# The third delta projection of a scan job, moved behind the group sum on TensorE

## The chip, the cores and the metric

One core of a Trainium2 chip runs the whole network in one launch. The metric is the device time of that launch in microseconds. Three runs of the kernel before took 19326.3, 19345.53 and 19361.93 us; their median, 19345.53 us, is the time before.

## The reference, cut to what matters

The network has four layers. Three kinds of selective scan (Mamba) fill nearly all of its time: layer 0 (causal Mambas over whole images), layers 1 and 2 (scans of an image in four directions) and layer 3 (Mambas along rows and columns). Each of them computes, for every channel d and each of N = 16 states n, a recurrence along the tokens:

```
xdbl  = xc @ xpW.T                      # rank (6 or 12) delta rows, 16 B rows, 16 C rows
delta = softplus(dt @ dtW.T + dtB)      # the delta projection and its softplus
def step(h, t):
    d_t, u_t, b_t, c_t = t
    h = exp(d_t[..., None] * A) * h + (d_t * u_t)[..., None] * b_t[:, None, :]
    return h, sum(h * c_t[:, None, :], axis=-1)      # the sum over states
```

Batch 4, 48 x 48 tokens, 192 model channels, 384 channels inside a Mamba; all arithmetic is fp32. Around the scans stand input projections, short convolutions, gates, output projections, norms, a small convolution block between layers 0 and 1 and an MLP at the end.

## The kernel before, in words

**Jobs and groups.** A scan is cut into jobs of CH = 384 tokens and 384 channels (a direction of layers 1 and 2 has 192 channels; its job puts 2 x 8 of the 16 states on the two halves of the 128 partitions, `parts` = 2). A job has three channel blocks i = 0, 1, 2 and works on NG = 4 states at a time; the unit of work is a group (job, i, g). In layers 0 and 3 a job has 3 x 4 = 12 groups (`MambaJob`), in layers 1 and 2 it has 3 x 2 = 6 (`DirJob`). `run_jobs` (line 775) is called three times: for 96 jobs of layer 0, 192 jobs of layers 1 and 2 (the *scan layers* below), and 96 jobs of layer 3. Each call has 1152 groups.

**What a group costs.** Five steps, one or two on each engine:
- `decay` (393): four exps on ScalarE, a = exp(delta A). For the first block it first starts the loads of the B and C rows (`fetch`). There are three decay buffers, so the decays of group t+3 wait until the scan of group t has read its own.
- `scan` (431) on VectorE: a product b = du x B (the row `inputs<-du,bcb`) and the scan proper (`h<-a,inputs`). `gather` (108) puts all of their waits in front of the product: for the decays, for the C/B rows, for the copy of `du` when g = 0 (`pools.entered`), and for the readers of the h buffer that is to be overwritten (`pools.readers`, `pools.weighed`). There are `hbufs` h buffers: 3 in layer 0, 4 elsewhere.
- `weigh` (457) on GpSimd: h times C, in place.
- `reduce` (472) on TensorE: four matmuls with an identity (or, for `parts` = 2, with a 128 x 64 matrix that adds the halves) sum h over states into the PSUM tile y. With g = 0 the skip terms go first (`skip`).
- `enter` (426) on ScalarE: the copy of du = delta x for the next block into PSUM, once per block. It is passed to `decay` as `between` and comes before the fourth exp.

**The loop.** In `run_jobs`, iteration t of the main loop (805 to 847) issues the scan of group t, the decays of t+2 (`ahead`), the copy of a finished y on ScalarE (`take`), the weighing of t, then one slot of the *stream*, the side work (norms of the finished images, `Side`), the gate and du products on GpSimd, and last the sum over states of group t-1 (`behind`):

```
        stream.run(at if at < per - 1 else per)
        ...
        if 0 <= t - behind < len(groups):
            job, i, g = groups[t - behind]
            job.reduce(i, g)
```

`at` is the position of group t in its job, from 0 to `per` - 1 (11 or 5). TensorE, GpSimd, ScalarE and VectorE run their instructions in the order of this code (`InOrder`, `in_order`); only the DMA issues of SyncE are placed by the scheduler.

**The stream.** While job n is scanned, `Stream` (710) works off the *units* of job n+1: input projection, convolution, B/C projection (`bc`), three delta projections, gates, and the output projection of job n-1. A unit is a matmul part (`pe`) and a ScalarE part (`act`), each with the slot at which it may be issued. `Stream.run(slot)` issues units in list order, at most two matmul parts ahead of their ScalarE parts, since the units share two PSUM tiles `ps`: the third delta matmul takes the tile that the first delta's softplus has read.

**The deltas.** `projections` (344) makes the units concerned. `delta(i)` (358) is one matmul of 12 or 6 rows (`ps<-bcd,dtT`) and one softplus (`delta<-ps,vec`). All three have the same slot: position 7 in layer 0 and in the first of each pair of jobs of layer 3, position 5 in the second of a pair (the twin), position 2 in the scan layers. Softplus and exp lie in different activation tables, so that a table load stands before the first softplus and another after the last.

Of the kernel before, what the change touches and what calls it, by code (L numbers as in the profile page):

```python
# [308 lines left out]
class ScanJob:  # L309
# [34 lines left out]
    def projections(self, xs, *slots):  # L344

        k, nc, w, pools = self.k, self.k.nc, self.w, self.pools
        nr = 2 * N + w.rank
        W = pools.W

        def bc(px):  # L350
            self.bcd = k.tile(pools.two, [nr, W], "bcd", 1)
            if self.entry is not None:
                k.g.memset(self.bcd[:, self.entry : self.entry + 1], 0.0)
            k.copy(self.bcd[:, self.tokens], px)
            self.bc = k.dram([2 * N, W], "bc")
            nc.sync.dma_start(self.bc, self.bcd[: 2 * N, :])

        def delta(i):
            def act(pd):
                if i == 0:  # L360
                    self.delta = k.tile(pools.two, [128, 3, CH], "delta")
                k.act(self.delta[:, i, :], pd, AF.Softplus, bias=w.dtb[:, i, :])

            return self.unit(
                slots[1],
                128,
                lambda ps: (ps, [(w.dtT[2 * N : nr, i, :], self.bcd[2 * N : nr, self.tokens])]),
                act,
            )

        first = self.unit(
            slots[0],
            nr,
            lambda ps: (ps, [(w.xpT[:, i, :], xs()[: pools.wide, i, :]) for i in range(3)]),
            bc,
        )
        return first, [delta(i) for i in range(3)]

    def fetch(self, g):

# [394 lines left out]
def run_jobs(jobs, side=None):  # L775

    ahead, behind, taken, gated, driven = 2, 1, 2, 3, 3  # L780
    last_group = jobs[0].pools.groups - 1
    groups = [(job, i, g) for job in jobs for i in range(3) for g in range(last_group + 1)]
    per = len(groups) // len(jobs)

    def at_group(t, g):

        if 0 <= t < len(groups) and groups[t][2] == g:
            return groups[t][:2]

    def offer(job):  # L790
        if side is not None and job.steps is not None:
            side.waiting += job.steps()

    jobs[0].load()
    stream = Stream(jobs[0].units(None))
    for t in range(per):
        stream.run(t)
    for t in range(driven):
        if first := at_group(t, 0):
            first[0].drive(first[1])  # L800
    jobs[0].enter(0)
    for job, i, g in groups[:ahead]:
        job.decay(i, g)
    stream = Stream([])
    for t in range(len(groups) + gated):
        n, at = divmod(t, per)
        if at == 0:
            last = jobs[n - 1] if n else None
            if n + 1 < len(jobs):
                jobs[n + 1].load()  # L810
                stream = Stream(jobs[n + 1].units(last))
        if at == per - ahead:
            stream.run(at - 1)
        if at == taken + 3 and n + 1 == len(jobs) and n:
            Stream(jobs[n - 1].outputs(*[(0, 0)] * 3)).run(per)
        if t < len(groups):
            job, i, g = groups[t]
            job.scan(i, g)
        coming = at_group(t + 1, 0)
        if t + ahead < len(groups):  # L820
            job, i, g = groups[t + ahead]
            job.decay(i, g, (lambda: coming[0].enter(coming[1])) if coming else None)
        if done := at_group(t - taken, last_group):
            done[0].take(done[1])
        if t < len(groups):
            if t + 1 < len(groups):
                job, i, g = groups[t + 1]
                job.carry(i, g)
            job, i, g = groups[t]
            job.weigh(i, g)  # L830
        stream.run(at if at < per - 1 else per)
        if t < len(groups):
            for slot, extra in jobs[n].extras:
                if slot == at:
                    extra()
        if side is not None and t < len(groups):
            if n and at == jobs[n - 1].offered:
                offer(jobs[n - 1])
            side.slot(at)
            side.end()  # L840
        if done := at_group(t - gated, last_group):
            done[0].gate(done[1])
        if begun := at_group(t + driven, 0):
            begun[0].drive(begun[1])
        if 0 <= t - behind < len(groups):
            job, i, g = groups[t - behind]
            job.reduce(i, g)
    Stream(jobs[-1].outputs(*[(0, 0)] * 3)).run(per)
    offer(jobs[-1])

# [118 lines left out]
def layer0(k, pairs, wh, norm, outs):  # L969
# [3 lines left out]
    with ExitStack() as ctx:  # L973
# [60 lines left out]
        for i in range(2):  # L1034
            jobs[n + i * NCH - NCH + 1].extras = ws[1][i].extras()
        run_jobs(jobs, side)


# [329 lines left out]
def scan_layers(k, pool, layers, ends, ahead):  # L1368
# [4 lines left out]
    with ExitStack() as ctx:  # L1373
# [9 lines left out]
        for n, (weights, src) in enumerate(layers):  # L1383
            ws, diag = weights.ws, weights.diag
            steps = ends[n](normed, pool)
            for b in range(B):
# [21 lines left out]
                late = scan(2, 0)  # L1408
        passes.append(late)
        run_jobs([job for p in passes for job in p], side)  # L1410
        scans.close()
        normed.alone = True
# [162 lines left out]
def row_mambas(k, weights, sets):  # L1575

    with ExitStack() as ctx:
        pools = ScanPools(k, ctx, 1, True)  # L1580
        jobs = []
        for (there, back), (srcs, outs, prior) in zip(weights.pairs, sets):
            if jobs:

                jobs[-2].extras = [(1, there.enter)]
            for b in range(B):
                for c in range(NCH):
                    of = None, srcs[b], outs[b]
                    last = prior[b] if prior is not None else None
                    first = MambaJob(k, pools, there, c * CH, False, *of)  # L1590
                    jobs += [
                        first,
                        MambaJob(k, pools, back, c * CH, True, *of, twin=first, prior=last),
                    ]
        run_jobs(jobs)
# [277 lines left out]
```

## Time and profile before

| of the profiled execution | |
|---|---|
| span | 19325.4 us (the three timed runs: 19326.3 to 19361.93) |
| busy: TensorE, VectorE, ScalarE, GpSimd | 17368.5, 18080.4, 12819.5, 14759.7 us |
| product `inputs<-du,bcb` on VectorE | 3456 times, 1769 ns |
| scan `h<-a,inputs` on VectorE | 3456 times, 3359 ns |
| weighing `h<-h,bcb` on GpSimd | 3456 times, 3447 ns |
| exps `a<-delta,A` on ScalarE | 13824 times, 602 ns |
| softplus `delta<-ps,vec` on ScalarE | 1152 times, 579 ns |
| delta matmuls `ps<-bcd,dtT` on TensorE | 2304 records (two for each fp32 matmul), 550 ns |

By name: PE is TensorE (PEld its weight loads), DVE VectorE, ACT ScalarE, POOL GpSimd, SPq the queue of SyncE. Most rows of the profile have line L56 or L93, those of two helpers, so groups are told apart by their tiles, written out<-in. A fp32 matmul leaves two records in the trace: the sum over states of one group is eight records. Time in brackets in a timeline is the idle time of the engine before the row, with what ended it as the profile infers it; of several waits it names the one that came last by its own account.

Layer 0 lies at about 40 to 6160 us of the span, the convolution block at 6160 to 6630, the scan layers at 6630 to 12710, layer 3 at 12870 to 18870, and the MLP follows up to 19325.

### The profile page before, as it was taken

The numbers are of one execution on the slowest core, as the hardware profiler recorded it, in microseconds if no ns is written. First come the engines' busy times: TensorE is split into PE (matmuls) and PEld (weight loads), VectorE is DVE, ScalarE is ACT, GpSimd is POOL, SyncE is SP. The second block draws the span as 40 slices with busy tenths as digits, with TensorE's granted clock in tenths as the row PEclk, the third lists the DMA queues.
The fourth block names the chain that finished last, engine by engine and source line by source line (L and its number), as shares of the span: only waits on it lengthen the run. The fifth ranks groups of instructions, "written<-read, shape, count | busy, mean of one in ns | idle before, by whom it ended". The sixth has DMA issues, their size and how long they took to land.

```text
span 19325.4 us, 162699 instructions
## 1 busy us (share of the span) xinstructions
PE 17368.5 (90%) x48240; PEld 8258.1 (43%) x48240; DVE 18080.4 (94%) x7297; ACT 12819.5 (66%) x22582; POOL 14759.7 (76%) x10860
## 2 busy tenths in 40 slices
PE   8999999999998888888888888889999999999999
PEld 4544545444444323333333333334444444444444
DVE  9999999999998699999999999969999999999993
ACT  6767777666665466676666777766666666666663
POOL 7888888878886288888888888857777777777770
PEclk9999999999999989999999999989999999999999
DMA  3333333323332366666666666633222332333231
GB/s 116 117 118 111 120 117 120 119 102 119 108 113 89 99 139 142 152 147 150 153 146 147 140 150 148 142 109 110 107 106 104 107 112 105 109 110 112 103 108 47
DMA packets 500500, 2306.55 MB, mean 119 GB/s; under 512 B 76664, under 2 KB 334304, under 8 KB 347168
## 3 DMA queue, kind: packets, MB, share of 16 engines
q1 hardware_dynamic: 499616, 2296.14, 41.9%
q8 instruction: 387, 6.34, 0.1%
q14 instruction: 497, 4.07, 0.1%
HBM read 2103.60 MB, written 192.32 MB: 119 GB/s over the span
## 4 chain that ended last, share of the span: by engine, by line
DVE 41%; POOL 32%; PE 13%; issue 9%; ACT 3%; DMA 2%; SPq 0%; POOLq 0%; DVEq 0%; ACTq 0%
DVE h L56 27%; POOL h L56 25%; DVE inputs L56 14%; PE y L56 6%; PE ps L56 4%; POOL dus L56 2%; PE vps L128 2%; POOL state L56 1%; ACT a L93 1%; DMA bcb<-bc 1%; POOL yt L56 1%; POOL bcb L56 1%; PE mop L128 1%; PE mps L128 1%; POOL nx L56 1%
## 5 line engine op out<-in xcount | busy, mean ns | idle before, releaser
L56 POOL TENSOR_TENSOR h<-h,bcb 128x1536 f32<-128x1536 f32 x3456 | 11912.3, 3447 | 1595.4 <-DVE h L56 1136.8
L56 DVE TENSOR_TENSOR_SCAN h<-a,inputs 128x1540 f32<-128x1540 f32 (+1 forms) x3456 | 11607.0, 3359 | 145.2 <-DVE inputs L56 1.4
L93 ACT ACTIVATE a<-delta,A 128x384 f32<-128x384 f32 (+1 forms) x13824 | 7417.2, 602 | 2662.1 <-DVE h L56 2642.6
L56 PE MATMUL y<-h,ident 128*128 128x384 f32 x18432 | 6727.0, 513 | 441.3 <-POOL h L56 438.0
L56 DVE TENSOR_TENSOR inputs<-du,bcb 128x1540 f32<-128x1540 f32 (+1 forms) x3456 | 6112.7, 1769 | 413.2 <-ACT a L93 116.9
L56 PEld LDWEIGHTS y<-h,ident 128*128 128x128 f32 x18432 | 3606.7, 200 | 3400.0 <-POOL h L56 868.6
L56 PE MATMUL y<-h,sum 128*64 128x384 f32 x9216 | 3642.2, 545 | 513.4 <-POOL h L56 386.7
L56 PEld LDWEIGHTS y<-h,sum 128*64 128x64 f32 x9216 | 1287.2, 149 | 2806.9 <-issue 1803.5
L56 POOL COPY state<-h 128x4 f32<-128x4 f32 x2304 | 434.4, 189 | 1920.5 <-DVE h L56 1899.9
L56 PE MATMUL ps<-xh,diag 128*128 128x384 f32 x4032 | 1418.4, 491 | 171.5 <-ACT xc L93 171.4
L56 PE MATMUL ps<-u,inT 96*128 96x384 f32 x3456 | 1250.4, 492 | 165.1 <-ACT z L93 120.7
L56 PE MATMUL ps<-bcd,dtT 12*128 12x384 f32 (+1 forms) x2304 | 1019.2, 550 | 352.5 <-ACT delta L93 349.4
L56 PEld LDWEIGHTS ps<-xh,diag 128*128 128x128 f32 x4032 | 750.2, 189 | 766.0 <-ACT xc L93 259.6
L93 ACT ACT_TABLE_LOAD x794 | 1018.7, 1283 | 14.0
L90 ACT ACT_TABLE_LOAD x789 | 1012.3, 1283 | 14.1 <-PEq L1863 0.7
L56 PEld LDWEIGHTS ps<-u,inT 96*128 96x128 f32 x3456 | 647.5, 190 | 674.7 <-ACT z L93 199.0
L93 ACT ACTIVATE delta<-ps,vec 128x384 f32<-128x384 f32 x1152 | 633.1, 579 | 309.1 <-PE ps L56 301.6
L56 PE MATMUL ps<-yt,outT 128*96 128x384 f32 x2304 | 789.7, 486 | 0.4 <-POOL yt L56 0.4
L56 PEld LDWEIGHTS ps<-bcd,dtT 12*128 12x128 f32 (+1 forms) x2304 | 382.6, 192 | 921.3 <-ACT delta L93 586.9
L93 ACT ACTIVATE du<-dus 128x384 f32<-128x384 f32 x1152 | 556.8, 483 | 139.3 <-DVE inputs L56 133.9
L56 POOL TENSOR_TENSOR dus<-delta,xc 128x384 f32<-128x384 f32 x576 | 575.4, 999 | 48.6 <-ACT delta L93 48.6
L93 ACT ACTIVATE o<-ps 96x384 f32<-96x384 f32 x288 | 140.3, 487 | 700.5 <-PE ps L56 700.5
(131 smaller groups left out, 9688.5 us busy)
## 6 DMA issues: line engine op xcount, KB each, us to landing
bcb<-bc SPq DMA_DIRECT2D x384, 1540.0 KB
bcb<-bc SPq DMA_DIRECT2D x768, 770.0 KB
bcb<-bc SPq DMA_DIRECT2D x384, 1536.0 KB
y<-o SPq DMA_DIRECT2D x192, 288.0 KB
xs<-xi_wh SPq DMA_DIRECT2D x96, 288.0 KB
xs<-xi_hw SPq DMA_DIRECT2D x96, 288.0 KB
added<-y SPq DMA_DIRECT2D x96, 288.0 KB
xs<-x_wh SPq DMA_DIRECT2D x96, 288.0 KB
```

Source lines behind the costliest of these rows:

```text
L56: return lambda *a, **kw: self.tc.keep_in_program_order(op(*a, **kw))
L90: self.in_order(self.nc.scalar.preload_act_table_set(LOG_EXP))
L93: return self.in_order(self.nc.scalar.activation(out, in_, func, **kw))
L128: ins = (engine or self.nc.tensor).matmul(out, lhsT, rhs, start=start and i == 0, stop=stop and i == n - 1)
```

## The change

The third delta unit of each job gets a slot half a position later than the other two, and the stream is run once more in each iteration, at `at + 0.5`, after `reduce`. So the third delta matmul is issued behind the sum over states of group t-1 instead of before it, and its softplus is issued after it in the program. In the built program 381 delta matmuls change places with the four (with a skip term, five or more) matmuls of a sum on TensorE; the lists of VectorE, ScalarE and GpSimd hold the same instructions in the same order as before; on SyncE some loads (`prior`, `xs`, `added`, the B/C rows) stand one or a few places earlier or later. The three jobs that come first in a call of `run_jobs` keep their order.

```diff
-        def delta(i):
+        def delta(i, at):
+
             def act(pd):
                 if i == 0:
                     self.delta = k.tile(pools.two, [128, 3, CH], "delta")
                 k.act(self.delta[:, i, :], pd, AF.Softplus, bias=w.dtb[:, i, :])
 
             return self.unit(
-                slots[1],
+                at,
                 128,
                 lambda ps: (ps, [(w.dtT[2 * N : nr, i, :], self.bcd[2 * N : nr, self.tokens])]),
                 act,
...
-        return first, [delta(i) for i in range(3)]
+        return first, [delta(i, slots[1]) for i in range(2)] + [
+            delta(2, tuple(s + 0.5 for s in slots[1]))
+        ]
...
             job, i, g = groups[t - behind]
             job.reduce(i, g)
+        stream.run(at + 0.5 if at < per - 1 else per)
     Stream(jobs[-1].outputs(*[(0, 0)] * 3)).run(per)
     offer(jobs[-1])
```

## The prediction, as put on record

> **What bounds the kernel now.** I read the busy times first, then a table by stage, then timelines of one job in each stage.
>
> ```profile
> PE 17368.5 (90%) x48240; PEld 8258.1 (43%) x48240; DVE 18080.4 (94%) x7297; ACT 12819.5 (66%) x22582; POOL 14759.7 (76%) x10860
> ```
> ```profile
> 100.00:6150.00 6050.00, 5613.42 (x16182) 2970.34 (x16183) 5841.62 (x2278) 4173.38 (x7340) 4995.31 (x4158) 0.97 0.32 114
> 6620.00:12700.00 6080.00, 5253.35 (x13645) 1877.52 (x13643) 5904.41 (x2302) 4210.16 (x7634) 5026.05 (x4285) 0.92 0.67 146
> 12860.00:18550.00 5690.00, 5203.65 (x14711) 2768.86 (x14711) 5584.15 (x2182) 3755.87 (x6469) 4352.32 (x2198) 0.95 0.30 108
> ```
>
> The columns are stage, length, then busy us of PE, PEld, DVE, ACT, POOL. VectorE sets the pace: a group costs it 1.77 + 3.36 us and 0.07 of spacing, 5.20 us, and it does nothing else in the scans. So only its idle time counts. Taken gap by gap from the timeline, by the position of the group in its job, gaps over 0.15 us come to: layer 0, 108.7 us in front of position 9 (75 of 95 jobs) and 23 us elsewhere; scan layers, 38.9 at position 1, 19.2 at 0, 17.8 at 4, 7.1 at 2; layer 3, none beyond its start.
>
> Layer 0, TensorE around position 7, whose product starts at 2040.88, and VectorE behind it:
>
> ```profile
> 2041.48 2.75 PE L56 MATMUL y<-h,ident 128*128 128x384 f32 x8
> 2044.16 1.55 PE L56 MATMUL ps<-bcd,dtT 12*128 12x384 f32 x4
> 2046.55 0.91 PE L56 MATMUL ps<-bcd,dtT 12*128 12x384 f32 x2 [0.84 <-ACT delta L93]
> 2047.38 7.12 PE L56 MATMUL y<-h,ident 128*128 128x384 f32 x16
> ```
> ```profile
> 2047.88 3.36 DVE L56 TENSOR_TENSOR_SCAN h<-a,inputs 128x1540 f32<-128x1540 f32 x1
> 2052.09 1.77 DVE L56 TENSOR_TENSOR inputs<-du,bcb 128x1540 f32<-128x1540 f32 x1 [0.85 <-ACT a L93]
> ```
>
> The third delta matmul waits for the first softplus, and the sums behind it wait with it. The sixteen records are the sums of positions 6 and 7; the first eight run at half pace (4.54 us against 2.75). With three h buffers, position 9 overwrites what sum 6 reads. The row names ScalarE, but in the stalled jobs the product starts 0.17 us after the modelled end of sum 6, job after job, so it is this sum that it waited for.
>
> Scan layers, one job, position 2 starting at 8026.00:
>
> ```profile
> 8028.15 1.28 ACT L93 ACT_TABLE_LOAD   x1
> 8029.45 1.05 ACT L93 ACTIVATE delta<-ps,vec 128x384 f32<-128x384 f32 x2
> 8031.03 0.58 ACT L93 ACTIVATE delta<-ps,vec 128x384 f32<-128x384 f32 x1 [0.53 <-PE ps L56]
> 8031.63 1.28 ACT L90 ACT_TABLE_LOAD   x1
> 8032.92 1.63 ACT L93 ACTIVATE a<-delta,A 128x384 f32<-128x384 f32 x3
> 8034.46 0.47 ACT L93 ACTIVATE du<-dus 128x384 f32<-128x384 f32 x1
> ```
> ```profile
> 8027.33 1.55 PE L56 MATMUL ps<-bcd,dtT 6*128 6x384 f32 x4
> 8030.08 0.91 PE L56 MATMUL ps<-bcd,dtT 6*128 6x384 f32 x2 [1.20 <-ACT delta L93]
> 8030.92 4.49 PE L56 MATMUL y<-h,sum 128*64 128x384 f32 x8
> ```
> ```profile
> 8036.40 1.77 DVE L56 TENSOR_TENSOR inputs<-du,bcb 128x1540 f32<-128x1540 f32 x1
> ```
>
> Here the third softplus has something urgent right behind it on ScalarE: table load, three exps, and the du copy of the next block, which ends at 8034.93. Position 4 needs it at 8036.40. The cover is 1.47 us (median over the jobs 1.47, a tenth of them under 0.12).
>
> [...] the softplus starts 0.02 us after the load. I use 1.28. [...]
>
> **The change, part by part.** Nothing is added or removed: the 381 delta matmuls and softplus and the table loads are as many as before, and the lists of ScalarE, GpSimd and VectorE are unchanged. What moves is the third delta matmul behind a sum, and in time its softplus with all that stands behind it on ScalarE. Times below count from the start of the product at the deltas' position.
>
> *Layer 0, gain.* Deltas 0 and 1 take 3.28 to 4.83. Sum 6 then starts there (its h is weighed at 3.74) instead of at 6.5, 1.7 us earlier. And it should run at full rate[...]. [...] With the start moved and every duration kept, gaps of 5 us remain; at full rate none. If all sums ran wholly at half rate, 34 would remain. I take a gain of 105 less 5 for waits elsewhere that have less slack: **-100** (-70 to -108).
> What is late instead: third softplus at 8.5, table, four exps to 12.5, needed at 15.6; take and sum 8 end near 19.3, needed at 20.8. Both covered.
>
> *Scan layers, loss.* Deltas 0 and 1 end at 2.88 where they start earliest. Sum 1 must wait for the weighing of position 1, which ends at 3.74; so it starts at 3.80. The next matmul starts 2.73 later, at 6.53; the softplus 0.95 after that (4.08 to 5.03 in this stage's rows), at 7.48 instead of 5.03. From softplus to the end of du is 3.90 us in every job (8031.03 to 8034.93), so du ends at 11.38, and with 0.06 for the hand-over position 4 starts at 11.44 instead of 10.40: VectorE stands for 1.04 us at the least. Doing this with each job's own start of the deltas (median 2.2, a quarter over 2.9) gives 279 us over 191 jobs (1.46 each) with all sums at full rate; 458 (2.40 each) with the sum durations of before; 713 with all at half rate. Half rate should be rarer than before[...]. I take 1.8 each, 344. From this goes what was stalled at position 4 already (17), and most of the waits for C/B rows at position 1, whose loads are issued before the new stall and land while VectorE stands (39, I take 30); side norms on ScalarE come about 1 us later relative to position 0, where 16 jobs already wait (+20). **+317** (+220 to +460).
>
> *Layer 3.* No VectorE gap to win. Deltas at position 5 or 7, du copies two iterations away, four h buffers: the delayed exps end at 12 to 15 where 15.6 is the limit. **0** (0 to +15).
>
> *SyncE.* Loads of `prior`, `xs` and `added` trade places with their neighbours. The trace shows 24 us of VectorE waits put down to DMA and 35 to the C/B copies in the scan layers: I take 0 and bound it by +-40.
>
> Sum: -100 + 317 + 0 = +217 on the span of 19325.4, 19542. The span lies 20 us under the median of the runs, so **19560 us**.
>
> **The rivals.**
> *A, faster.* The du copy stays covered in the scan layers and layer 0 gains alone: 19345 - 105 = 19240. It decides where the stall at position 4 averages under 105/191 = 0.55 us, that is if the third softplus slips by less than 2.0 us there. For it: a cover of 1.47. Against: the weighing ends at 3.74 in nearly all jobs and eight records take 2.7, which no order can shorten: 2.45.
> *B, much slower.* The new idle spell behind the third delta in the scan layers (6.5 to the next sum, which waits for `take` behind the exps, near 12.5) keeps TensorE at half rate more often, and sum 1 with it: 713 - 27 - 100, 19930. Against: sum 0, weighed by -1.46, comes between.
> *C, a draw.* The loss is near its floor and much of it falls on stalls that exist: 200 - 56 at position 4, 1 and 0, less 105: +39, 19385. Against: half of the jobs start their deltas too late for the floor.
>
> **How the numbers follow.** Forecast, slower by 115 to 390: 0.82. A 0.05, B 0.06, C 0.07. Ends: full rate everywhere, 279 - 17 - 39 - 108 = +115 (19460); old durations, 458 - 17 + 20 - 70 = +391 (19736). The range is 19450 to 19720. A measurement of this kernel tells 0.2%, 39 us, from no change; slower by more: forecast, B and part of C, 0.90; within, the rest of C, 0.05; faster, A, 0.05.
>
> **What would show it.** Layer 0: the gap before position 9 gone, sum 6 in eight records over 2.75 us, starting at 4.83. Scan layers: gaps of 1 to 3 us in front of position 4 of nearly every job, released by the du copy; third softplus at 7.5 or later; the gaps at position 1 smaller. Layer 3 as before. I am wrong if ScalarE waits for TensorE at the third softplus and position 4 still starts at 10.40, or if the gap at position 9 stays.

## The result, and the profile after

The changed kernel takes 19770.97 us (median of four runs, 19770.45 to 19773.47) against 19335.92 us of the kernel before in the same comparison: a ratio of 1.0216, 95% interval 1.0204 to 1.0228. It is slower by 435 us. Slower was forecast, but by 217 us, and the time lies 51 us above the range of 19450 to 19720.

The busy line of the page of the changed kernel, and below it the table by stage (stage, length, then busy us of PE, PEld, DVE, ACT, POOL, the granted clock of TensorE, the busy share of the DMA engines and what they moved in GB/s; the stages are cut at their own ends here):

```profile
PE 17302.4 (88%) x48240; PEld 8210.5 (42%) x48240; DVE 18079.3 (91%) x7297; ACT 12760.6 (65%) x22582; POOL 14743.3 (75%) x10860
```
```profile
100.00:6110.00 6010.00, 5547.92 (x16177) 2937.99 (x16175) 5837.48 (x2276) 4165.82 (x7340) 4986.47 (x4156) 0.98 0.33 115
6610.00:13140.00 6530.00, 5301.69 (x13622) 1921.30 (x13622) 5889.06 (x2297) 4162.98 (x7605) 5008.08 (x4276) 0.88 0.61 136
13330.00:19300.00 5970.00, 5386.42 (x15409) 2836.18 (x15408) 5870.70 (x2295) 3904.69 (x6768) 4579.88 (x2309) 0.97 0.30 107
```

Every engine has the work of before; the added time is idle time of VectorE, and nearly all of it is in the scan layers, where the clock of TensorE also fell from 0.92 to 0.88. From the first to the last scan of each stage: layer 0, 6115 to 6079 us (-36); scan layers, 6070 to 6549 (+479); layer 3, 5992 and 5992. The small difference of layer 0 has to be read with care: the same layer 0 as before, in the run only_dir below, took 6142 us, 27 more than in the profile of before, so the gain lies between 36 and 63 us. Gaps of VectorE over 0.15 us, by the position in the job in front of which they lie, in us:

| | before | after |
|---|---|---|
| layer 0, position 9 | 108.7 | 13.4 |
| layer 0, positions 0, 5, 10 | 0, 10.9, 5.6 | 29.4, 27.7, 18.5 |
| scan layers, position 4 | 17.8 | 438.7 |
| scan layers, positions 0, 1, 2 | 19.2, 38.9, 7.1 | 72.7, 13.1, 45.1 |

The list of waits of VectorE (total us, times, longest) is now led by a row that was far down in it. First the row of before, then that of the change:

```profile
DVE inputs L56 <- ACT du L93: 42.6, 35, 2.7
```
```profile
DVE inputs L56 <- ACT du L93: 567.5, 291, 4.6
```

In the scan layers 190 of the 191 gaps in front of position 4 end with the du copy.

The same job of layer 0 as in the prediction, TensorE and VectorE (its position 7 now starts at 2044.73):

```profile
2048.01 1.55 PE L56 MATMUL ps<-bcd,dtT 12*128 12x384 f32 x4
2049.50 2.85 PE L56 MATMUL y<-h,ident 128*128 128x384 f32 x8
2052.28 0.91 PE L56 MATMUL ps<-bcd,dtT 12*128 12x384 f32 x2
2053.72 2.85 PE L56 MATMUL y<-h,ident 128*128 128x384 f32 x8 [0.54 <-POOL h L56]
```
```profile
2055.13 1.77 DVE L56 TENSOR_TENSOR inputs<-du,bcb 128x1540 f32<-128x1540 f32 x1
2056.93 3.36 DVE L56 TENSOR_TENSOR_SCAN h<-a,inputs 128x1540 f32<-128x1540 f32 x1
2060.84 1.77 DVE L56 TENSOR_TENSOR inputs<-du,bcb 128x1540 f32<-128x1540 f32 x1 [0.54 <-POOL bcb L56]
```

Sum 6 starts 4.77 us after the product of position 7, at full rate, and position 9 (2055.13) no longer waits. But position 10 does, for a copy on GpSimd: one of the small gaps that took back most of the gain.

The same job of the scan layers (position 2 now starts at 8084.98), ScalarE, TensorE and VectorE:

```profile
8088.42 1.05 ACT L93 ACTIVATE delta<-ps,vec 128x384 f32<-128x384 f32 x2
8094.08 0.58 ACT L93 ACTIVATE delta<-ps,vec 128x384 f32<-128x384 f32 x1 [4.60 <-PE ps L56]
8094.68 1.28 ACT L90 ACT_TABLE_LOAD   x1
8095.97 1.63 ACT L93 ACTIVATE a<-delta,A 128x384 f32<-128x384 f32 x3
8097.51 0.47 ACT L93 ACTIVATE du<-dus 128x384 f32<-128x384 f32 x1
8097.92 0.60 ACT L93 ACTIVATE a<-delta,A 128x384 f32<-128x384 f32 x1
8098.42 0.47 ACT L93 ACTIVATE o<-y 64x384 f32<-64x384 f32 x1
```
```profile
8086.30 1.55 PE L56 MATMUL ps<-bcd,dtT 6*128 6x384 f32 x4
8088.76 4.40 PE L56 MATMUL y<-h,sum 128*64 128x384 f32 x8 [0.91 <-POOL bcd L56]
8093.09 0.95 PE L56 MATMUL ps<-bcd,dtT 6*128 6x384 f32 x2
8098.99 7.56 PE L56 MATMUL y<-h,sum 128*64 128x384 f32 x16 [4.95 <-issue]
```
```profile
8098.10 1.77 DVE L56 TENSOR_TENSOR inputs<-du,bcb 128x1540 f32<-128x1540 f32 x1 [2.75 <-ACT du L93]
```

Read them as one chain: sum 1 (8088.76) holds the third delta matmul until 8093.09, ScalarE stands 4.60 us for it, and the table load, three exps and the du copy follow; du ends at 8097.98, and VectorE starts position 4 at 8098.10, 2.75 us late. Then comes what I had not priced: `take` (`o<-y`) is behind the exps too, at 8098.42. The one PSUM tile y is free only when it has been copied, so sum 2 starts at 8098.99, after 4.95 us in which TensorE does nothing. It is so in all 191 jobs: the first matmul into the next y starts 0.05 to 0.10 us after `take` has ended.

### The profile page after: what moved, and what is told of

Read it like the earlier page. It is cut to its first block, busy times and chain, and to the rows that moved or that the text cites. A ratio compares the mean times of both kernels' runs of the same rounds, so it can differ in the third digit from the quotient of the medians.

```text
span 19769.7 us, 162583 instructions
## 1 busy us (share of the span) xinstructions
PE 17302.4 (88%) x48240; PEld 8210.5 (42%) x48240; DVE 18079.3 (91%) x7297; ACT 12760.6 (65%) x22582; POOL 14743.3 (75%) x10860
## 4 chain that ended last, share of the span: by engine, by line
POOL 38%; DVE 27%; PE 20%; issue 11%; ACT 3%; DMA 1%; POOLq 0%; SPq 0%; DVEq 0%; ACTq 0%
POOL h L56 30%; DVE h L56 18%; PE y L56 10%; DVE inputs L56 9%; PE ps L56 6%; POOL dus L56 3%; PE vps L128 2%; POOL state L56 2%; ACT a L93 1%; POOL bcb L56 1%; POOL yt L56 1%; ACT L90 1%; PE mop L128 1%; PE mps L128 1%; POOL nx L56 1%
## 5 line engine op out<-in xcount | busy, mean ns | idle before, releaser
L56 PE MATMUL y<-h,ident 128*128 128x384 f32 x18432 | 6659.1, 506 | 670.0 <-POOL h L56 666.3
L56 PEld LDWEIGHTS y<-h,ident 128*128 128x128 f32 x18432 | 3520.4, 196 | 3597.5 <-POOL h L56 1238.3
L56 PE MATMUL ps<-bcd,dtT 12*128 12x384 f32 (+1 forms) x2304 | 949.1, 518 | 2.5 <-ACT bcd L93 1.8
L56 PE MATMUL y<-added,ident 64*64 64x384 f32 x576 | 307.2, 620 | 513.5 <-ACT o L93 511.8
L56 PE MATMUL y<-xc,diagD 128*128 128x384 f32 x1152 | 527.0, 540 | 199.4 <-ACT yt L93 188.1
```

Source lines behind the costliest of these rows:

```text
L56: return lambda *a, **kw: self.tc.keep_in_program_order(op(*a, **kw))
```

## The experiments

My theory after the result: the loss is in the scan layers alone and has two ways, both through the queue of ScalarE behind the third softplus. (1) The du copy, which VectorE needs at position 4. (2) `take`: sum 2 waits for the y tile; in the profile of the change it starts 5.14 us (median) after its weighing and runs wholly or in part at half rate in 190 of 191 jobs (before: 1.83 us, 74 of 191); TensorE carries the delay into the next job, whose deltas start at 2.58 us (median) after position 2 instead of 2.18. (Not into every job: behind a job whose sums also take in an earlier result, `added`, the deltas start at 3.56 us on average against 2.82 before; behind the others TensorE has nearly caught up, 2.01 against 1.88.) The rivals: the loss comes from TensorE itself (its new order, its half rate), or from the loads that stand elsewhere on SyncE.

**Each part alone.** `parts` is 1 in layers 0 and 3 and 2 in the scan layers.

```diff
-            delta(2, tuple(s + 0.5 for s in slots[1]))
+            delta(2, tuple(s + (0.5 if pools.parts == 1 else 0) for s in slots[1]))
```

> The change in the jobs of layers 0 and 3 alone; the scan layers as before. My theory: the whole loss is in the scan layers, and layer 0 keeps the small gain that its stage shows in the profile of the change (6115 to 6079 us): 36 us under the kernel before, about 19300. Rival (the loss comes from the moved third delta wherever it is, layers 0 and 3 included, or from the loads that SyncE places elsewhere): no gain, 19336 or slower.

> The change in the jobs of the scan layers alone. My theory: 479 us over the kernel before, about 19815, slower than with the whole change, with gaps of 2.3 us on average before position 4 that end with the du copy. Rival (the parts act on each other): about 19770, the time of the whole change, or less.

The second has `parts == 2` in that line. Measured: the first 19305.23 us, ratio to the kernel before 0.9977 (0.9968 to 0.9987), its layer 0 at 6079 us as in the whole change; the second 19830.73 us, 1.0245 (1.0224 to 1.0265), its scan layers at 6554 us with 444 us of gaps before position 4. The parts add up, -47 and +478 us against +435: the loss is in the scan layers, and layer 0 has a small gain.

**The third softplus one iteration later.**

```diff
-            delta(2, tuple(s + 0.5 for s in slots[1]))
+            delta(2, (slots[1][0] + 0.5, slots[1][1] + (1 if pools.parts == 2 else 0.5)))
```

> The whole change, but in the scan layers the third softplus is issued one iteration later, behind the exps, the du copy and take (position 3 instead of 2.5); its matmul stays behind the sum. It costs two more table loads per job, 2.6 us of ScalarE, which has idle time there. My theory (what stalls VectorE is the du copy queued behind the third softplus on ScalarE): the gaps before position 4 go from 439 us to under 30 and take comes early again, so sum 2 runs on time; total 19290 to 19345. Rival (what stalls is TensorE: its new order and its half rate): gaps of 200 us or more stay, total over 19500.

Measured: 19265.84 us, ratio 0.9954 (0.9937 to 0.9971). The gaps before position 4 fell from 438.7 to 2.6 us, and the scan layers take 6040 us, 29 less than before the change; the time is 24 us below the range of the expectation. ScalarE in the same job (position 2 at 7985.96, position 4 at 7996.36):

```profile
7989.75 1.05 ACT L93 ACTIVATE delta<-ps,vec 128x384 f32<-128x384 f32 x2
7990.82 1.28 ACT L90 ACT_TABLE_LOAD   x1
7992.11 1.63 ACT L93 ACTIVATE a<-delta,A 128x384 f32<-128x384 f32 x3
7993.65 0.47 ACT L93 ACTIVATE du<-dus 128x384 f32<-128x384 f32 x1
...
7996.34 0.58 ACT L93 ACTIVATE delta<-ps,vec 128x384 f32<-128x384 f32 x1
```

The du copy ends at 7994.12, 2.24 us ahead of position 4, and the softplus follows where nobody waits for it. The order on TensorE is, record by record, still that of the change, and it costs nothing: the rival that lays the loss to TensorE falls. The rival of the loads is not settled by this run, because the scheduler put most of SyncE's issues back as well: of the 1951 in the scan layers 258 stand elsewhere in the change than before, and 31 in this run (78 in take_first and 75 in take_du_first, below). Two things speak against it. In the trace of the change VectorE waits for a load only once in the scan layers, in front of their first product; after that no engine waits for one longer than 0.6 us. And du_first, below, takes most of the gaps before position 4 away with all but 59 of these issues where the change has them. What stalled VectorE was the coupling on ScalarE.

**`take` ahead of the exps.** In `run_jobs`, for the scan layers:

```diff
+        early = jobs[0].pools.parts == 2
+        done = at_group(t - taken, last_group)
+        if done and early:
+            done[0].take(done[1])
         coming = at_group(t + 1, 0)
...
-        if done := at_group(t - taken, last_group):
+        if done and not early:
             done[0].take(done[1])
```

> The whole change, but in the scan layers the copy of a finished y (take) is issued ahead of the decays of its iteration instead of behind them. It puts 0.49 us more in front of the du copy in each job, 94 us in all. My theory of the second part of the loss (take behind the late exps keeps the one y tile, so sum 2 starts 5 us late and at half rate, TensorE lags into the next job, and its deltas start late): sum 2 starts near 1 us after its weighing, deltas start at 2.2 (median) or earlier instead of 2.6, gaps at positions 0 and 2 fall from 129 us to under 60; total 50 to 200 us under the whole change, 19570 to 19720. Rival (the late deltas come from the loads or the side work): sum 2 is early but the deltas start as late as before, and the total rises by about 94 us, to 19865.

Measured: 19663.59 us, ratio 1.0159 (1.0138 to 1.0179), 107 us under the whole change although every du copy has a further ScalarE instruction in front of it. Sum 2 starts 0.99 us after its weighing, the deltas at 1.57 us (median), the gaps at positions 0 and 2 fell from 118 to 19 us (to be read against the 129 of the expectation, which counts the spacing of all products). Way (2) exists and costs about what was expected; the gaps before position 4 stay (414 us), since way (1) is untouched. They did not shrink more although sum 1 now starts 0.74 us earlier on average: `take` puts 0.37 us in front of the du copy, and sum 1 is slower (3.34 us on average until the third delta, 3.10 in the change).

**The du copy ahead of the exps.** In `decay`:

```diff
-            if j == NG - 1 and between is not None:
+            if j == (0 if pools.parts == 2 else NG - 1) and between is not None:
```

> The whole change, but in the scan layers the du copy is issued ahead of the four exps of its iteration instead of ahead of the fourth. The third softplus and the table load still stand in front of it. My theory (VectorE waits for the du copy through the queue of ScalarE): du comes 1.62 us earlier, every gap before position 4 shrinks by that, 439 us to about 140, and the total goes from 19771 to about 19430. Rival (VectorE waits for TensorE, the du copy only ends last): little change, over 19650.

Measured: 19643.64 us, ratio 1.015 (1.013 to 1.0171). This expectation failed, twice. The table load is issued by the first exp, so the du copy went ahead of it too and gained 1.62 + 1.30 = 2.92 us, not 1.62. The gaps before position 4 did fall, from 439 to 130 us, but they should have gone to about 32 then. And the gaps at position 0 rose from 73 to 222 us. The deltas start at 4.09 us (median) now: `take` is still behind the exps, sum 2 starts 5.88 us after its weighing, and VectorE, which no longer stops at position 4, gives TensorE no time to catch up; waits at position 0 end with GpSimd's copies (103 us), the du copy (84 us) and `PE y` (32 us). I took this to be way (2) alone, and tried both edits together:

> The whole change, with both edits in the scan layers: take ahead of the decays, the du copy ahead of the four exps. My theory now (the loss has two ways through the queue of ScalarE: the du copy before position 4, and take, which keeps the one y tile and makes the sums late; du_first left the second, and its lag came out at position 0): the gaps before position 4 shrink by 1.62 each, 413 us to about 120, the gaps at position 0 stay under 30, sum 2 starts near 1 us after its weighing; total 19664 - 290 = 19370 (19330 to 19430). Rival (with VectorE no longer stopped at position 4, TensorE is short of time whatever take does): gaps of over 100 us at position 0 as in du_first, total over 19480.

Measured: 19269.2 us, ratio 0.9953 (0.9937 to 0.9969), below the range given, because I had again counted 1.62 us; with 2.92 the gaps of take_first before position 4 come to 14, and 15.7 were measured. Position 0 has 9 us, sum 2 starts 0.39 us (median) after its weighing. ScalarE in a job of this run, both copies now ahead of the table load:

```profile
7996.81 0.58 ACT L93 ACTIVATE delta<-ps,vec 128x384 f32<-128x384 f32 x1 [2.15 <-PE ps L56]
7997.28 0.47 ACT L93 ACTIVATE o<-y 64x384 f32<-64x384 f32 x1
7997.65 0.48 ACT L93 ACTIVATE du<-dus 128x384 f32<-128x384 f32 x1
7998.15 1.28 ACT L90 ACT_TABLE_LOAD   x1
```

With the third delta behind the sum, and its softplus where the change puts it, ScalarE's order decides between +479 and -20 us in the scan layers.

**Layer 0: does the half rate make the gaps?** The kernel before, in its own order on TensorE, ScalarE and GpSimd, with delta matmuls over 128 rows; the added weights are zero:

```diff
-        self.dtT = k.tile(pool, [nr, 3, 128], f"dtT{tag}")
+        self.dtT = k.tile(pool, [128, 3, 128], f"dtT{tag}")
+        nc.vector.memset(self.dtT, 0.0)
...
-            self.bcd = k.tile(pools.two, [nr, W], "bcd", 1)
+            self.bcd = pools.bcd
...
-                lambda ps: (ps, [(w.dtT[2 * N : nr, i, :], self.bcd[2 * N : nr, self.tokens])]),
+                lambda ps: (ps, [(w.dtT[:, i, :], self.bcd[:, self.tokens])]),
```

> The kernel before, with its order, but the delta matmuls run over all 128 rows instead of 12 or 6: the weights of the other rows are zero, and one zeroed tile is kept for the projected rows. The matmuls have the same number of columns and records. My theory ([...] the spell around the deltas halves the rate of sum 6 in layer 0, and that makes the gaps before position 9): no half-rate spans start at position 8, sum 6 takes 2.7 to 2.9 us, the gaps before position 9 go from 109 us to under 15; total 19230 to 19260. Rival (the time of the idle spells counts and the rows do not, or the late start of the sum makes the gaps): the gaps stay over 60 us, total over 19290.

Measured: 19272.95 us, ratio 0.9959 (0.9944 to 0.9974). The gaps before position 9 fell from 108.7 to 13.9 us, the half-rate time of the stage from 348 to 48 us, and layer 0 from 6115 to 6043 us. TensorE in the same job (position 7 at 2030.40, position 9 at 2040.80, on time):

```profile
2033.59 1.45 PE L56 MATMUL ps<-bcd,dtT 128*128 128x384 f32 x4
2036.07 0.91 PE L56 MATMUL ps<-bcd,dtT 128*128 128x384 f32 x2 [1.03 <-ACT delta L93]
2036.82 5.43 PE L56 MATMUL y<-h,ident 128*128 128x384 f32 x16
```

The third delta still waits for the first softplus and the sums still wait for it, 1.03 us here. But the sixteen records take 5.43 us instead of 7.12, and no product is late. So the late start alone did no harm (sum 6 starts 6.42 us after position 7, 6.50 before); the half rate did, and with 128 rows instead of 12 in the delta matmuls it was nearly gone: the granted clock from 100 to 6080 us was 1.00, 0.97 before. The total is 13 us above the expected range: the scan layers took 6093 us, 23 more than in the kernel before, of which I can't say more than that the same scan layers took 6070 and 6081 us in two profiles (before, only_mamba).

**What layer 0 lost again.** softplus_next with `take` ahead of the exps in layers 0 and 3 (`parts == 1` in the edit above), and softplus_next with the 128 rows:

> As softplus_next, and in layers 0 and 3 take is issued ahead of the decays of its iteration. My theory of what layer 0 lost again (the third softplus now delays the exps of two groups, take behind them, and sum 8 and the gate matmuls, partly at half rate, so the gates and the du copy for position 0 are late): the gaps before position 0 of layer 0 go from 33 us to under 10, total about 19240. Rival (the gaps at position 0 come from the gates themselves): no change, about 19266.

> softplus_next with the delta matmuls over all 128 rows. My theory: with the clock kept up, the late gates of layer 0 (gaps before position 0, 33 us) and the slow sums of the scan layers go; total 19215 to 19245, under both full_rows and softplus_next. Rival (the row count does not act on the clock): as softplus_next, 19266.

Measured: 19229.82 us (0.9937, 0.9921 to 0.9954) and 19221.85 us (0.9933, 0.9919 to 0.9948). In the first, the gaps over 0.15 us at position 0 of layer 0 fell from 31.5 to 5.2 us and at position 5 from 28.5 to 12.7; layer 0 takes 6037 us. In the second, position 0 has 3.9 us and layer 0 takes 6048. Both bear out that the late gates came from `take` and the half-rate spell behind the moved delta (with the 128 rows the granted clock of the whole run is 0.975, in softplus_next 0.957). The 13 and 18 us at positions 9 and 10 stay in both.

> The third delta behind the sum, its softplus one iteration later in the scan layers, take ahead of the decays in layers 0 and 3, and delta matmuls over 128 rows. My theory: each takes away gaps that the others leave; layer 0 near 6040, scan layers near 6037, total 19200 to 19222, against 19230 and 19222 of the two pairs. Rival: what is left are gaps that end with the state copies of GpSimd and with loads, which none of the three touches; no gain over the pairs, 19222 to 19235.

Measured: 19218.93 us, ratio 0.9929 (0.9912 to 0.9945). That is inside what the theory gave, but only 3 us under the better pair, with which the rival's range begins; the runs of either scatter by more. Three edits together beat both kernels, but the third one adds nothing that can be told.

## Why the prediction was right or wrong

- *VectorE sets the pace, only its gaps count:* right. The span grew by 444 us, VectorE's busy time not at all.
- *Layer 0, the gap before position 9 goes:* right in mechanism and size. It fell by 95 us (123 against only_dir, whose layer 0 is that of before); sum 6 starts at 4.77 (4.83 forecast) and runs at full rate; that it would was only an estimate of mine. full_rows shows that the half rate was the cause.
- *"less 5 for waits elsewhere that have less slack":* wrong by 37 to 64 us; layer 0 gained 36 to 63, not 100. Two things stand behind it. I wrote that `take` and sum 8 are covered, and in all but two jobs they are (sum 8 ends at 20.15, median, where I had 19.3), but I did not go on to what follows sum 8 on TensorE: the gate matmuls, their gates on ScalarE, and the du copy for position 0, whose cover was 0.95 us. It now ends up to 1.05 us after the scan in front of position 0 (29 us of gaps; next_and_take and full_rows_next take them away). And the gaps at positions 9 and 10 end with GpSimd's copies, in jobs where GpSimd has one more product in front of the copy: that of a side norm at position 9 (all 20 gaps), the addition of an earlier output (`o<-o,prior`) at position 10 (all 39). full_rows, with the old order, has the same gaps. They had been hidden by VectorE's stop at position 9.
- *Scan layers, the du copy loses its cover:* right in mechanism; every one of the 191 jobs has the gap, and softplus_next, which takes the softplus out of the way, removes it. The smallest gap is 0.96 us, close to the floor of 1.04 that I had worked out.
- *The size of it, 1.8 us a job:* this is the term that failed first. It measured 2.30, 95 us more over the stage. Above the floor of 1.04, the length of sum 1 beyond 2.73 us is 0.37 (3.10 on average), about the 0.34 that I had allowed; the hand-over from the du copy to VectorE is 0.12 in the stalled jobs where I had 0.06; and the start of sum 1 after 3.80 is 0.82 (4.62 on average) where I had 0.42, because I took *"each job's own start of the deltas"* from the trace of before as if the change could not move it. It moves by way of `take`, the single y tile and sum 2. In softplus_next and take_du_first, where `take` is early again, sum 1 starts at 4.23 and 4.20, as I had it. I had seen that spell: rival B names it, and I dismissed it with *"sum 0, weighed by -1.46, comes between"*. That sum does come between, but it comes late. B was half right: in the change not the rate of sum 1 suffers (from its start to its end 3.82 us on average before, 3.17 now; wholly or in part at half rate in 111 of 191 jobs before, in 43 now) but the time at which it starts.
- *+20 at position 0, nothing at position 2:* this failed in the same way. They grew by 53 and 38 us, 71 more than I had; take_first removes 99 of the 118. *-30 at position 1:* -26.
- *Layer 3 unchanged:* right, within 0.4 us.
- *SyncE +-40:* not tried alone. That the loads cost little is read from the trace of the change, as said under softplus_next; a small effect stays possible.
- *What would show it:* gaps of 1 to 3 us before position 4, released by the du copy, the third softplus at 7.5 or later (8.96 median), smaller gaps at position 1: all came, with some gaps longer, up to 4.98 us. Rivals A and C are refuted by the 438.7 us at position 4. My range also ended at 19720, below the +391 (19736) that I had worked out for its slow end; the measured time lies above both.

So the sign and both main mechanisms were right, and the sum lay 226 us under what the stages lost: about 95 at position 4, 71 at positions 0 and 2, and 64 in layer 0, of which up to 27 may be scatter of the profile of before. But for the gaps that had been hidden, these are follow-up costs of one kind: an instruction that becomes late delays all that is queued behind it, not only the first that someone waits for.

## What to carry to other kernels

When an instruction is moved later on one engine, walk down the queue of the engine that consumes it, past the first urgent instruction to the next ones, and ask of each what waits for it; here the copy that frees the only accumulator was the second. Starts and idle spells read from the old trace are inputs only as long as the change does not move them. Where two engines are coupled like this, the cheap repair is in the order of the consumer: issuing the late softplus after the urgent copies turned +435 us into -87.

## What the runs showed of the hardware

In these runs the granted clock of TensorE changed with the rows that the matmuls use. full_rows has the matmuls of the kernel before in the same order, with 128 rows instead of 12 or 6 in those of delta. From 100 to 6080 us of the span, in layer 0, TensorE was busy no longer than before (5477 us against 5562), and its granted clock was 1.00 against 0.97; the half-rate time of the stage fell from 348 to 48 us. Over the profiled execution the clock was 0.969 against 0.944. A second pair differs in these rows too: full_rows_next had 0.975, softplus_next 0.957. How the clock comes to fall in a given spell was not shown. The whole kernel became 0.4% faster, with multiplications by zero.
